# Layer 1's cross-attention: its first tiles placed away from the filler's memory, a norm in two halves, a third staging buffer, and a 2 MB load and two table loads moved

## The chip, the core and the metric

The kernel runs on one NeuronCore of a Trainium2 chip. The metric is device time in microseconds (us) of one execution: the median of three runs before the change is 2085.6 us (2083.99 to 2086.98). Five engines work side by side: TensorE (PE, with its weight loads shown as PEld), VectorE (DVE), ScalarE (ACT), GpSimd (POOL) and SyncE (SP), which here only issues DMAs. ACT and POOL issue DMAs too, each on its own queue (SPq, ACTq, POOLq in the profile).

## The reference

Four layers, each a cross-attention and a feed-forward network (FFN) with eight experts, on a residual `x` of 2 x 512 rows of 256, with a context of 2 x 1024 rows:

```python
x = x + L0_xattn(layernorm(x), ctx)
x = x + L0_ffn(layernorm(x))          # 8 experts, the best one per row, FFN 1024
x = x + L1_xattn(ctx, layernorm(x))   # 8 heads of 64
x = x + L1_ffn(layernorm(x))          # 8 experts of 512, and a shared one
x = x + L2_xattn(layernorm(x), ctx)
...
```

The change lies around layer 1's attention. Its reference, cut:

```python
def L1_xattn(x, latents, gamma_x, beta_x, gamma_l, beta_l, Wq, Wkv, Wo):
    xn = layer_norm(x, gamma_x, beta_x)          # the context
    ln = layer_norm(latents, gamma_l, beta_l)    # the residual, normalised a second time
    q = ln @ Wq
    k_x, v_x = split(xn @ Wkv)                   # 1024 rows of each batch
    k_l, v_l = split(ln @ Wkv)                   # 512 rows of each batch
    k = concat([rope_rotate(k_x), k_l])
    v = concat([v_x, v_l])
    return softmax(q * 64**-0.5 @ k.T) @ v @ Wo
```

So the keys and values of the context (`k_x`, `v_x`) depend on nothing but the inputs, and can be computed at any time before; the queries and 512 of each batch's keys and values need the residual that layer 0's FFN leaves.

## The kernel before

The residual `X` stays in SBUF as eight tiles of 128 rows (`[128, 8, 256]`, tiles 0 to 3 are batch 0). All matmuls are float32. Instructions are ordered by a scheduler that works on the program order and on dependencies; a call of `behind(x, y)` pins x behind y in an engine's stream. The scheduler also sees to the memory: a tile of a new pool that takes over the memory of an older tile waits for the older one's last use.

**Layer 0's FFN** (L1247 to L1301) routes the rows to experts. The function `moe` runs over pairs of slot tiles: indirect DMAs on POOL gather rows (`xs`, L648) and scatter results (`yd`, L660), PE computes `pa`, `pg`, `y`, and expert weights `w` arrive on SP's, ACT's and POOL's queues into the pool `L0g` (`ep`, four buffers).

**The filler.** Beside this FFN PE computes the keys and values of layer 1's context: `ahead1` makes, for each batch, 16 jobs (8 of keys, then 8 of values). A job is four matmuls of 128x512 from the transposed context `cT` and the weights `wkv` into a PSUM tile `pk` (L190 is the line of the helper `mm2`), a copy by ACT into a staging tile (`sk` for keys, L880; `sv` for values, L902; one tag with two buffers), and a 256 KB store that ACT issues into HBM (`kd`, `vd`). All 16 jobs of batch 0 run in `first_batch`, before the first pair; of batch 1, six run as `between` the pairs and ten behind the last pair (L1298).

**The end of the FFN.** Behind the ten jobs the results come back: four loads `yg` of 256 KB on SP (L831), eight additions into `X` on DVE (L868).

**Layer 1's attention** (L1302 to L1490) opens three pools, `L1c`, `L1k` and `L1t`, on the memory that the FFN's pools leave, the filler's `cT` and staging tiles among it. It normalises the eight tiles (`norm_of` twice: statistics on DVE L81, L82, square root on ACT L69, reciprocal on DVE L72; then `norm_to` L107 writes `xn`), transposes them on PE (16 transposes, L175, four to a PSUM tile) and scales them into `xT` on DVE or ACT (L182, L184). Then it runs over eight groups (batch, pair of heads). `fetch(n)` loads a group's keys `kT`, a copy with its halves exchanged (`turned`, four DMAs from `exchange`, L214) and values `v`; `prep(n)` is a generator that adds the residual's keys (`pk`), values (`pv`) and queries (`pq`, `qT`); `rotate` applies the rotary tables: DVE multiplies `turned` by the sine (L205), POOL multiplies `kT` by the cosine and adds (L206, L207). A stream of 6 steps a group follows: scores (`s`, L1367), maximum (`nm`, L1371), exp (`p`, L1374), transposes (L1388) and products (`o`, L1397). Small work is shared out between the steps as `pieces`.

**Later.** `cTr` is the transposed context that layer 2 reads, 2 MB; its load stands behind the definitions for later layers (L1898), and the scheduler issues it on SP behind `yg` and ahead of `fetch(0)`. In layer 1's FFN (L1894 to L1949) `sqrt_table()` is a small square root whose purpose is to have ACT's table of square roots loaded; it stands ahead of the keys and values for layer 2 (`keys16`, `values16`). ACT holds one table at a time: a change of function of another table shows as ACT_TABLE_LOAD.

## Time and profile before

| what | before |
|---|---|
| median of three runs | 2085.6 us |
| lowest and highest | 2083.99 and 2086.98 us |
| the profiled execution | 2082.45 us |
| its span, from first to last instruction | 2080.7 us |
| mean granted clock of TensorE | 0.978 |
| instructions | 29514 |
| HBM read and written | 232.70 and 24.82 MB |

The span is the profiled execution without the 1.75 us that lie around it. The page gives the busy time of each engine, then the span in 40 slices of 52 us; a digit is the busy share in tenths:

```profile
PE   7999999998998999999899899899999999999996
...
PEclk9999999999999999999999999899979999999998
DMA  4111111129884211100327241478300100289882
```

Counted from 0, slices 9 to 12 (468 to 676 us) hold the first filler batch, layer 0's FFN and the last ten jobs, slices 13 to 19 layer 1's attention. PEclk is the clock that TensorE was granted, in tenths. The places of the change, with their times in the trace:

| place | us |
|---|---|
| first batch of the filler, 16 jobs | up to 518 |
| last ten jobs of the filler | 647.5 to 669.2 |
| loads of yg issued | 651.04 to 653.9 |
| load of cTr issued | 654.09 |
| first load of kT issued | 669.29 |
| transposes of xn | 669.94 to 676.3 |
| first scores of attention 1 | 681.37 |
| layer 1's FFN, first expert load issued | 1015.48 |
| table load for the norm ahead of layer 2 | 1177.15 |

In lines of waits, "A <- B: t, n, l" says that the instruction group A stood idle for t us in n times, l the longest, until B ended.

### The profile page before, as it was taken

To read this page: it belongs to the slowest core of one execution; us is meant where nothing else is said; L and a number is where in the kernel's file an instruction comes from. 1 tells how busy PE (TensorE), PEld (TensorE's weight loads), DVE (VectorE), ACT (ScalarE), POOL (GpSimd) and SP (SyncE) were. 2 spreads that over 40 slices of the span, in tenths; PEclk is the share of its full clock that TensorE was granted. 3 is DMA by queue.
4 is the path that set the end of the run, shared out by engine and by line. 5 is a ranking of instruction groups with operands and counts; after the bars stand their busy time and mean duration, and the time that the engine had idled before them with its cause. 6 is when DMAs were issued, how large, how long until landed. Compare 5 with 4: busy or idle time off the path is not lost. (4 is left out here: it accounts for less than half of the span.)

```text
span 2080.7 us, 29514 instructions
## 1 busy us (share of the span) xinstructions
PE 1976.3 (95%) x11294; PEld 1147.5 (55%) x11294; DVE 1040.0 (50%) x2018; ACT 864.9 (42%) x1693; POOL 506.1 (24%) x500
## 2 busy tenths in 40 slices
PE   7999999998998999999899899899999999999996
PEld 3444444433666454555458644599833333488994
DVE  7666666782113566666531466410167767332223
ACT  4444444433112666656411344322225545624433
POOL 2132333310211212211213222453242311122220
PEclk9999999999999999999999999899979999999998
DMA  4111111129884211100327241478300100289882
GB/s 142 42 33 35 35 36 31 31 92 325 357 336 144 78 39 43 42 21 1 122 95 253 89 181 28 150 277 328 142 11 20 30 18 21 75 315 371 349 320 87
DMA packets 87911, 267.64 MB, mean 129 GB/s; under 512 B 23120, under 2 KB 55248, under 8 KB 79312
## 3 DMA queue, kind: packets, MB, share of 16 engines
q1 hardware_dynamic: 69040, 144.36, 20.9%
q0 software_dynamic: 10656, 106.57, 13.4%
q10 hardware_dynamic: 8064, 14.68, 1.9%
q8 instruction: 96, 1.57, 0.3%
q14 instruction: 55, 0.45, 0.1%
HBM read 232.70 MB, written 24.82 MB: 124 GB/s over the span
## 5 line engine op out<-in xcount | busy, mean ns | idle before, releaser
L1769 ACT ACTIVATE p<-s 128x512 f32<-128x512 f32 (+3 forms) x384 | 186.9, 545 | 154.5 <-PE s L1768 103.2
L1709 PE MATMUL s<-kT,qT 32*128 32x512 f32 (+3 forms) x768 | 201.8, 603 | 5.8 <-DVE mx L1718 1.9
L1768 PE MATMUL s<-qA,kT 32*128 32x512 f32 (+3 forms) x768 | 195.2, 593 | 0.5 <-DVE nm L1713 0.3
L1718 DVE TENSOR_REDUCE mx<-s 128x1 f32<-128x512 f32 x256 | 165.5, 694 | 53.3 <-PE s L1709 33.9
L190 PE MATMUL pa<-sT,w 128*128 128x128 f32 x1536 | 185.7, 275 | 0.8 <-issue 0.5
L190 PEld LDWEIGHTS pa<-sT,w 128*128 128x128 f32 x1536 | 181.6, 192 | 5.6 <-issue 2.8
L772 PE MATMUL y<-w,hT 128*128 128x256 f32 x768 | 175.9, 381 | 2.9 <-DVE hT L768 2.0
L1374 ACT ACTIVATE p<-s,nm 128x512 f32<-128x512 f32 x192 | 129.3, 686 | 80.9 <-DVE nm L1371 80.9
L1188 ACT ACTIVATE p<-s 128x1024 f32<-128x1024 f32 x128 | 124.1, 1021 | 89.8 <-PE s L1183 89.8
L207 POOL TENSOR_TENSOR kT<-kT,turned 128x512 f32<-128x512 f32 x62 | 100.9, 1634 | 226.2 <-DVE turned L205 198.4
L1189 DVE TENSOR_SCALAR p<-p 128x1024 f32<-128x1024 f32 x128 | 106.8, 842 | 96.2 <-ACT p L1188 96.2
L772 PEld LDWEIGHTS y<-w,hT 128*128 128x128 f32 x768 | 141.6, 190 | 22.2 <-DVE hT L768 3.2
L1371 DVE TENSOR_REDUCE nm<-s 128x2 f32<-128x1024 f32 x96 | 113.2, 1221 | 80.3 <-PE s L1367 80.3
L1194 DVE TENSOR_TENSOR acc<-acc,p 128x1024 f32<-128x1024 f32 x96 | 132.6, 1381 | 2.8
L768 DVE TENSOR_TENSOR hT<-act,pg 128x512 f32<-128x512 f32 x58 | 39.9, 687 | 177.5 <-PE pg L190 165.2
L1112 PE MATMUL o<-p,v 128*64 128x512 f32 x512 | 124.9, 606 | 2.6 <-DVE p L1189 2.6
L1183 PE MATMUL s<-qT,kT 64*128 64x512 f32 x512 | 127.2, 615 | 0.0
L660 POOL DMA_INDIRECT yd<-yo,slot_to x60 | 59.6, 993 | 264.8 <-ACT yo L819 124.1
L206 POOL TENSOR_TENSOR kT<-kT,cos 128x512 f32<-128x512 f32 x62 | 87.8, 1427 | 118.7 <-DMA turned<-kT 71.3
L1388 PEld LDWEIGHTS pt<-ident,p 128*128 128x128 f32 x768 | 84.1, 141 | 53.0 <-issue 20.0
L190 PE MATMUL pg<-sT,w 128*128 128x128 f32 x928 | 113.1, 275 | 0.0
L648 POOL DMA_INDIRECT xs<-xd,slot_of x60 | 57.8, 963 | 214.7 <-PE pt L654 124.5
(364 smaller groups left out, 3162.3 us busy)
## 6 DMA issues: line engine op xcount, KB each, us to landing
w<-in_L_experts_dram SPq DMA_DIRECT2D x8, 3200.0 KB
w<-in_L_experts_dram SPq DMA_DIRECT2D x6, 3072.0 KB
w<-in_L_experts_dram SPq DMA_DIRECT2D x8, 2048.0 KB
w<-in_L_experts_dram SPq DMA_DIRECT2D x8, 1536.0 KB
turned<-kT SPq DMA_DIRECT2D x60, 128.0 KB
kd<-sk ACTq DMA_DIRECT2D x28, 256.0 KB
yg<-yd SPq DMA_DIRECT2D x24, 256.0 KB
vd<-sv ACTq DMA_DIRECT2D x16, 256.0 KB
```

The lines of the kernel that those rows point to most:

```text
L190: nc.tensor.matmul(ps_ap, lhsT[:, dc, lcols], rhs[:, dc, rcols], start=(dc == 0), stop=(dc == 1))
L772: x = nc.tensor.matmul(y, hT[:, f, :], w2[:, f, :], start=(f == 0), stop=(f == FT - 1)).ins
L1112: nc.tensor.matmul(G[n]["o"][64 * j : 64 * j + 64, :], V[g, b][:, kt, pr * P + 64 * j : pr * P + 64 * j + 64], p[:, j, :], start=(kt == 0) ...
L1183: nc.tensor.matmul(s1[:, j, :], G[n]["kT"][r, kt * P : (kt + 1) * P], G[n]["qT"][r, :], start=True, stop=True)
L1188: last_exp[0] = nc.scalar.activation(p, s1, AF.Exp, scale=0.125).ins
L1194: nc.vector.tensor_add(G[n]["acc"], G[n]["acc"], p)
L1371: nc.vector.tensor_reduce(nm[:, qt, :, c], s1, AX.X, ALU.max, negate=True)
L1374: nc.scalar.activation(p[:, j, :], s1[:, j, :], AF.Exp, bias=nm[:, qt, j, c : c + 1], accum_out=l[:, qt, j, c : c + 1],)
L1709: nc.tensor.matmul(s1[:, :w], qT[r, qt * P : (qt + 1) * P], kT[r, c * 512 : c * 512 + w], start=True, stop=True)
L1718: G[n]["max"] = nc.vector.tensor_reduce(mx[:, qt, j, c : c + 1], s1, AX.X, ALU.max).ins
L1768: nc.tensor.matmul(s2[:, qs], kT[r, kt * P : (kt + 1) * P], qA[r, qs], start=True, stop=True)
L1769: G[n]["exp"] = nc.scalar.activation(p[:, j, qs], s2[:, qs], AF.Exp, scale=0.25).ins
```

## The change

- `ahead`/`ahead1`: the staging tag has three buffers for layer 1's keys and values (layer 2's keys keep two).
- Layer 0's FFN: the expert weights' pool is closed ahead of the pools around it. The attention's pools `L1c` and `L1k`, and a pool for `cTr`, are opened inside the FFN's scope on that memory (right side), while the filler's `cT` and staging tiles still live.
- The last ten jobs of the filler are split into nine and one. Between them, in program order, tiles 0 to 3 get their results, are normalised (`norm_of(X, 0, 4)`, `norm_to`) and transposed into `xT`; the last job is pinned behind these transposes on PE. Then tiles 4 to 7 get their results and their statistics.
- The other half's `norm_to` and transposes become `second_rows()`, three pieces in the attention's second step. The norm and the 16 transposes ahead of the attention are gone.
- `exp_table` loads ACT's table of exponentials behind the last square root of that norm. In layer 1's FFN `sqrt_table` stands behind `values16`, pinned behind the last copy of results.
- `cTr` is loaded behind the loads of `fetch(1)`, in the attention's first step.

```diff
@@ -62,11 +62,13 @@
             reason="order of the stream",
         )
 
+    scaled = [None]
+
     def recip_sqrt(src, n, scale, eps, after=None):
 
         r = small.tile([P, n], F32, tag=f"rsq{n}", name="rsq")
         nc.vector.tensor_scalar(r, src, scale, eps, ALU.mult, ALU.add)
-        x = nc.scalar.activation(r, r, AF.Sqrt).ins
+        x = scaled[0] = nc.scalar.activation(r, r, AF.Sqrt).ins
         if after is not None:
             behind(x, after)
         nc.vector.reciprocal(r, r)
@@ -157,6 +159,11 @@
             reason="order of the stream",
         )
 
+    def exp_table(after):
+
+        junk = small.tile([P, 1], F32, tag="junk", name="junk")
+        behind(nc.scalar.activation(junk, ones[:, 0:1], AF.Exp).ins, after)
+
     def layernorm(dst, src, n, twice=False):
         norm_to(dst, src, norm_of(src, 0, n, twice))
 
@@ -164,17 +171,17 @@
         for _ in turn_blocks(*args, **kw):
             pass
 
-    def turn_blocks(ps, dst, src, n, g=None, b=None, tag="mm", first=0):
+    def turn_blocks(ps, dst, src, n, g=None, b=None, tag="mm", first=0, **kw):
 
 
         for blk in range(first, n // 4):
             pair = ps.tile([P, 2, 512], F32, tag=tag, name="pt", bufs=2) if tag == "s" else None
             for dc in range(2):
-                pt = pair[:, dc, :] if tag == "s" else ps.tile([P, 512], F32, tag=tag, name="pt")
+                pt = pair[:, dc, :] if tag == "s" else ps.tile([P, 512], F32, tag=tag, name="pt", **kw)
                 for i in range(4):
-                    nc.tensor.transpose(
+                    x = nc.tensor.transpose(
                         pt[:, i * P : (i + 1) * P], src[:, blk * 4 + i, dc * P : (dc + 1) * P], ident
-                    )
+                    ).ins
                 to = dst[:, dc, blk * 512 : (blk + 1) * 512]
                 if g is None:
                     nc.scalar.copy(to, pt)
@@ -182,7 +189,7 @@
                     nc.vector.tensor_scalar(to, pt, g[:, dc : dc + 1], b[:, dc : dc + 1], ALU.mult, ALU.add)
                 else:
                     nc.scalar.activation(to, pt, AF.Identity, bias=b[:, dc : dc + 1], scale=g[:, dc : dc + 1])
-                yield
+                yield x
 
     def mm2(ps_ap, lhsT, lcols, rhs, rcols):
 
@@ -816,7 +823,7 @@
         return yd
 
     def plain(yo, y, *ws):
-        nc.scalar.copy(yo, y)
+        last_act[0] = nc.scalar.copy(yo, y).ins
 
     def results(pool, yd, t0, n, to=(None, None)):
 
@@ -875,7 +882,7 @@
             if job[0] == "k":
                 _, kd, j, col, cols, c0 = job
                 mm2(pk, w, cols, src, slice(c0, c0 + 512))
-                k = st.tile([P, 512], F32, tag="sk", name="sk", bufs=2)
+                k = st.tile([P, 512], F32, tag="sk", name="sk", bufs=2 if w.shape[2] == D else 3)
                 if bias is None:
                     nc.scalar.copy(k, pk)
                 else:
@@ -898,7 +905,7 @@
         def values(pv, kt):
             r = slice(b * S + kt * P, b * S + (kt + 1) * P)
             mm2(pv, cT, r, w, slice(512, 1024))
-            v = st.tile([P, 512], F32, tag="sk", name="sv", bufs=2)
+            v = st.tile([P, 512], F32, tag="sk", name="sv", bufs=3)
             nc.scalar.copy(v, pv)
             stored.append(nc.scalar.dma_start(vds["L1"][r, :], v).ins)
             stores.append(stored[-1])
@@ -944,7 +951,7 @@
         ahead(ps, None, None, None, [("v", n) for n in range(B * nkt // 2)], values)
         return copies
 
-    last_product = [None]
+    last_product, last_act = [None], [None]
 
     def value_tiles(pool, nkt):
 
@@ -1244,12 +1251,14 @@
     rw1 = load_rows(state, d["L1_ffn_router_wT"], "rw1")
     spread = load(pp, [P, P], d["c_spread"], "spread")
 
+    att = ExitStack()
     with (
         tc.tile_pool(name="L0f", bufs=1, reuse_waits="tile") as fp,
         tc.tile_pool(name="L0h", bufs=2, reuse_waits="tile") as hp,
-        tc.tile_pool(name="L0g", bufs=4, reuse_waits="tile") as ep,
         psum(2, "L0fps") as ps,
     ):
+        weights0 = ExitStack()
+        ep = weights0.enter_context(tc.tile_pool(name="L0g", bufs=4, reuse_waits="tile"))
         rb = load_bc(fp, d["L0_ffn_router_b"], "rb")
         xn = fp.tile([P, TT, D], F32, tag="xn", name="xn")
         mv = small.tile([P, TT, 2], F32, tag="mv8", name="mv")
@@ -1295,21 +1304,35 @@
                 ahead1(ps, hp, wkv, cT, 1, slice(2 * s - 2, 2 * s))
 
         yd = moe("L0", ps, hp, ep, xn, slots, 1024, AF.Silu, True, plain, first_batch, None, between)
-        ahead1(ps, hp, wkv, cT, 1, slice(6, None))
+        ahead1(ps, hp, wkv, cT, 1, slice(6, 15))
         yg = fp.tile([P, TT, D], F32, tag="xn", name="yg")
-        for t0 in (0, 4):
-            add_results(results(fp, yd, t0, 4, [yg[:, t0 : t0 + 4, :]]), [mp], X, range(4))
-
+        weights0.close()
+        ctxr = ExitStack()
+        crp = ctxr.enter_context(tc.tile_pool(name="ctxr", bufs=1, side="right", reuse_waits="tile"))
+        cTr = crp.tile([P, 2, B * S], F32, tag="cTr", name="cTr")
+        cp = att.enter_context(tc.tile_pool(name="L1c", bufs=1, side="right", reuse_waits="tile"))
+        kp = att.enter_context(tc.tile_pool(name="L1k", bufs=2, side="right", reuse_waits="tile"))
+        xT = cp.tile([P, 2, NT], F32, tag="xT", name="xT")
+        xn = cp.tile([P, TT, D], F32, tag="oT", name="xn")
+        got = [results(fp, yd, t0, 4, [yg[:, t0 : t0 + 4, :]]) for t0 in (0, 4)]
+        add_results(got[0], [mp], X, range(4))
+        norm = norm_of(X, 0, 4, True)
+        norm_to(xn, X, norm)
+        turned = list(turn_blocks(ps, xT, xn, 4, g_l, b_l))[-1]
+        start = len(nc.cur_bb.bb.instructions)
+        ahead1(ps, hp, wkv, cT, 1, slice(15, None))
+        for x in list(nc.cur_bb.bb.instructions)[start:]:
+            if x.engine == mybir.EngineType.PE:
+                behind(x, turned)
+        add_results(got[1], [mp], X, range(4))
+        norm = norm_of(X, 4, 4, True)
+        exp_table(scaled[0])
 
     with (
-        tc.tile_pool(name="L1c", bufs=1, reuse_waits="tile") as cp,
-        tc.tile_pool(name="L1k", bufs=2, reuse_waits="tile") as kp,
+        att,
         tc.tile_pool(name="L1t", bufs=2, reuse_waits="tile") as tmp,
         psum(1, "L1ps") as ps,
     ):
-        xT = cp.tile([P, 2, NT], F32, tag="xT", name="xT")
-        to_T(ps, xT, normed(cp, True, "oT"), TT, g_l, b_l, "s")
-
         wts = [cp.tile([P, 4, P], F32, tag=f"wt{i}", name=f"wt{i}") for i in range(2)]
         for w in wts:
             nc.gpsimd.memset(w, 0.0)
@@ -1351,9 +1374,15 @@
             kd = kds["L1"][n * P : (n + 1) * P, :]
             nc.sync.dma_start(kT[:, 0:S], kd)
             exchange(turned, kd, 32, 64)
-            nc.sync.dma_start(
+            return nc.sync.dma_start(
                 v[:, 0:8, :], vds["L1"][b * S : (b + 1) * S, pc].rearrange("(t p) f -> p t f", p=P)
-            )
+            ).ins
+
+        def second_rows():
+
+            norm_to(xn, X, norm)
+            yield
+            yield from turn_blocks(ps, xT, xn, TT, g_l, b_l, first=1, bufs=3)
 
         def scores(n, u):
             c, qt = u // 4, u % 4
@@ -1464,6 +1493,8 @@
 
 
             n, w = divmod(t, 6)
+            if t == 1:
+                pieces.add(second_rows(), 3)
             if n < len(groups):
                 for k in range(2):
                     scores(n, 2 * w + k)
@@ -1483,7 +1514,9 @@
                 if u == 5:
                     pieces.add(end(m), 2, True)
             if n + 1 < len(groups) and w == 0:
-                fetch(n + 1)
+                x = fetch(n + 1)
+                if n == 0:
+                    behind(nc.sync.dma_start(cTr, d["ctxT"].rearrange("(t p) f -> p t f", p=P)).ins, x)
             for k in range(4):
                 pieces.share(24 - 4 * w - k if n < len(groups) else 1)
                 if 0 < t <= 6 * len(groups):
@@ -1893,9 +1926,6 @@
 
     frp = ctx.enter_context(tc.tile_pool(name="front", bufs=1, reuse_waits="tile"))
     rw2 = load_rows(frp, d["L2_ffn_gate_wT"], "rw2")
-    ctxr = ExitStack()
-    crp = ctxr.enter_context(tc.tile_pool(name="ctxr", bufs=1, side="right", reuse_waits="tile"))
-    cTr = load_rows(crp, d["ctxT"], "cTr")
     pre, pp, loads, params = params16("L2", False, True)
     V = value_tiles(pp, 4)
 
@@ -1940,9 +1970,9 @@
         for t in range(TT):
             nc.vector.tensor_scalar(xn[:, t, :], xn[:, t, :], top[:, t : t + 1], None, ALU.mult)
         yd = moe("L1", ps, hp, ep, xn, slots, 512, AF.Silu, True, plain, shared)
-        sqrt_table()
         keys16(ps, fp, "L2", wk, bk, 4)
         copies = values16(ps, wv, 4, V)
+        sqrt_table(last_act[0])
         yg = fp.tile([P, TT, D], F32, tag="xT", name="yg")
         norm = landed(results(fp, yd, 0, 4, [yg[:, 0:4, :]]), None, copies[1])
         add_beside(results(fp, yd, 4, 4, [yg[:, 4:8, :]]), None)
```

## The prediction

> **What bounds the kernel now.** I read the page first: TensorE (PE) is busy for nearly the whole span, so only stretches in which it idles, or runs at half clock, can pay.
>
> ```profile
> PE 1976.3 (95%) x11294; PEld 1147.5 (55%) x11294; DVE 1040.0 (50%) x2018; ACT 864.9 (42%) x1693; POOL 506.1 (24%) x500
> ```
>
> Then the busy time by stretch (first figure: length; then each engine; last three: granted clock, DMA share, GB/s) around what the change touches: the last third of the first filler batch (485 to 520), the rest of layer 0's FFN (to 647), the seam into attention 1 (647 to 682), the attention.
>
> ```profile
> 485.00:500.00 15.00, 11.62 (x32) 4.61 (x31) 0.72 (x6) 2.34 (x4) 4.03 (x4) 1.00 0.90 309
> 500.00:520.00 20.00, 15.64 (x42) 5.29 (x42) 0.42 (x1) 6.22 (x10) 0.95 (x1) 1.00 0.92 310
> ...
> 545.00:647.00 102.00, 99.37 (x660) 76.27 (x656) 16.11 (x27) 15.24 (x29) 16.03 (x17) 1.00 0.71 291
> 647.00:660.00 13.00, 12.49 (x29) 5.62 (x30) 4.78 (x14) 4.21 (x6) 0.54 (x1) 1.00 0.72 245
> 660.00:671.00 11.00, 7.44 (x15) 2.73 (x13) 4.99 (x23) 3.25 (x7) 1.13 (x2) 0.84 0.58 207
> 671.00:682.00 11.00, 10.03 (x42) 5.88 (x44) 4.16 (x9) 4.03 (x6) 5.26 (x4) 0.84 1.05 303
> ...
> 700.00:1000.00 300.00, 299.25 (x1632) 156.67 (x1630) 193.01 (x262) 188.01 (x481) 51.55 (x39) 1.00 0.10 29
> ```
>
> The attention leaves 0.75 of 300 us idle: what starts it earlier ends it earlier, and what is put into it is paid in full. Two places have slack: the first batch (35 − 27.26 = 7.74 us idle) and the seam. The waits there (total us, times, longest), for the seam and then the batch:
>
> ```profile
> SPq L1352 <- PE pk L190: 14.6, 1, 14.6
> ```
>
> ```profile
> POOL wt L1315 <- PE pk L190: 21.7, 1, 21.7
> ...
> ACT sv L902 <- DMA vd<-sv: 6.1, 5, 2.7
> ...
> DVE xn L107 <- PE pk L190: 3.0, 1, 3.0
> ```
>
> ```profile
> ACT sk L880 <- DMA kd<-sk: 16.3, 6, 6.2
> ...
> ACT sv L902 <- DMA vd<-sv: 5.6, 3, 2.6
> ACT sv L902 <- DMA kd<-sk: 4.4, 2, 2.5
> ```
>
> In the seam three first users of attention 1's pools (the first key load, the memset, the normalised rows) wait for the filler's last matmul, whose memory they take over. In both places ACT's copy waits for a store that still holds one of two staging buffers. TensorE's own time line at the seam (start, us, ... [idle before]):
>
> ```profile
> 665.69 3.46 PE L190 MATMUL pk<-wkv,cT 128*128 128x512 f32 x4 [2.49 <-ACT sv L902]
> 669.94 0.33 PE L175 MATMUL pt<-ident,xn 128*128 128x128 f32 x1 [0.79 <-DVE xn L107]
> ...
> 674.11 1.73 PE L190 MATMUL pk<-xT,wkv 128*128 128x512 f32 x2
> ...
> 676.97 1.95 PE L190 MATMUL pv<-wkv,xT 128*128 128x128 f32 x16
> 678.76 1.88 PE L190 MATMUL pq<-xT,wq 128*128 128x512 f32 x4
> 681.37 1.99 PE L1367 MATMUL s<-kT,qT 64*128 64x512 f32 x8 [0.73 <-POOL kT L206]
> ```
>
> **The seam, part by part.** I follow it from the filler's start at 647.5 to the first scores, 681.37 before.
>
> Filler. A job is four 128x512 matmuls: eight of them took 3.7 us, so 1.84 a job; nine were over at 662.61 + 0.59 = 663.2 with PE hardly idle, and the third buffer leaves them there. The tenth waited 2.49 for ACT's copy, which waited for a store, and then ran at half clock (0.43 to 0.86 a matmul); its last pair ended at 669.15.
>
> First half's norm. The four loads of yg are issued at 651.0 to 653.9 and their eight additions ran from 654.47 to 659.0. Four tiles need two loads, four additions (0.42 each) and four statistics (0.40 + 0.17): about 657.6, then Sqrt at 657.9. DVE now runs the other half's additions and three of its statistics before it uses that Sqrt (4×0.42 + 3×0.57 = 3.4), and the second Sqrt follows at some 661.7. Four xn (0.40 each) take 662.8 to 664.2; they no longer wait for the filler. The eight transposes, one behind each xn, end at 664.6, an idle spell of about 0.5. The tenth job, pinned behind them, ends at 664.6 + 1.8 = 666.4.
>
> Eviction, the step I trust least. On DVE the half's xT eviction stands behind the other half's last norm steps, two products of turned with sin (0.69 each) and four xn (1.6): about 668.4 to 669.2. On ACT it stands behind the third Sqrt, the Exp table load (1.28) and two copies (0.59 each): 667.7 to 668.5. So PE idles from 666.4 to 669.2.
>
> First group. pk, pv and pq took 1.73, 1.95 and 1.88 with half a group's clock lost; together 5.6, then qT 0.60 and the gap of 0.73: first scores at 669.2 + 5.6 + 1.3 = 676.1, which is 5.3 earlier. kT's rotation was the last wait before the scores; its loads are now issued at 654.5 instead of 669.3, right behind yg, so POOL (two pairs of 1.43 and 1.63) ends near 670 and leaves that wait.
>
> Moved into the attention: eight transposes, two evictions, four xn. Eight transposes took 1.1 (669.94 to 673.2 with waits, 0.60 for a clean four): 1.2 us paid in full. DVE has a third of its time free there (193 of 300), so the rest is hidden; without that cover the four xn and one eviction would cost 1.6 + 0.8.
>
> Clock. Half clock held from 665.29 to 668.70 and 672.11 to 675.53. The new 2.8 us idle is longer than the 2.49 that came with the first spell, so I count one spell of 3.41, of which half, 1.7, is lost; 1.1 of it is already in the three rows taken. 0.6 more. Seam: 5.3 − 1.2 − 0.6 = **3.5**. Ends: with DVE's eviction in ACT's place and no half clock, 5.3 + 0.7 + 1.1 − 1.2 = 5.9; with two spells and 2 us later loads, −0.2.
>
> The Trainium skill (TensorE: Matmul & The Clock Gate, "What's actually happening") puts the drop to half clock behind one idle window of about 3.4 us. The trace shows the 3.41 us as the length of a slow spell, but a spell that began with 2.49 us of idle. By the page the 2.8 us would cost no clock and the seam would gain 5.2; by the row, 3.5. The row decides.
>
> **cTr's 2 MB load** was issued at 654.09 ahead of the first key loads, and goes behind the second group's. SP's queue behind it (kT, turned ×4, v) and the stores of the filler share its DMA time: the share was 1.05 at 671 to 682. It is used first at 1165.4, in a stretch with DMA share 0.10; the cover is 480 us, its price 0. What SP issues after it, group 2's loads, comes six steps later.
>
> **Third staging buffer in the first batch.** PE needs 1.84 us a job, but copies come every 2.6 (488.89, 492.10, ... 517.48). With stores deeper in flight the copies could follow PE: all 7.7 us back at most. But the DMA engines are at 0.90 and 0.92, loading 12 MB of expert weights between the stores, so only 0.10×15 + 0.08×20 = 3.1 us of their time is unused. Lower end 0: stores just wait longer. I take **3.0**, nearer the DMA's row. From 520 to 647 PE idles 0.91 + 2.63 us only, so what is won is carried to 647.5. Pair 1's weights landed near 527.5 for a start at 532.76; they hang on the same stores and come earlier with them, and the between jobs' waits could give 0 to 1.
>
> The Trainium skill (DMA: Bandwidth & Descriptors, "Issuing engines are not separate DMA queues") says that transfers of SP, ACT and GpSimd run on the same 16 engines and interleave. That speaks against the buffer: by it the gain ends at the 3.1 of unused share; by ACT's wait alone, 7.7.
>
> **Tables and order elsewhere, 0.** Exp: the load (1.28 at 681.29) lay under scores and maxima; exp came at 683.80 after DVE's maximum. Uncovered it costs 1.28, and in its new place it is already in ACT's chain above. Sqrt before layer 2: the load (1.28 at 1177.15) moves to where ACT idles 2.25, but norm_to also waited 0.66 for PE: 0 to 0.3 gained. Layer 1's FFN: before, two 1.5 MB expert loads stood first on SP, at 1015.48 (9.15 with a wait for POOL) ahead of the shared gate at 1024.73. Now gate, up and down go first, behind the weights' matmul at 1020.5, and down is rid of its wait for po (issued 1031.61). Three expert loads instead of two follow the xd stores at 1045 to 1047; 4.5 MB at the batch's 310 GB/s is 14.5 us, over by 1063, and the first routed tile comes near 1100 at DMA share 0.04. Uncovered: 5 us.
>
> Sum: 3.5 + 3.0 = 6.5. The profiled execution was 2082.45 (span 2080.7, 1.75 around it): 2075.95. It lies 3.15 below the median 2085.6, to which I apply the same difference: **2079.1**.
>
> **Rivals.** Differences under 0.2%, 4.2 us, are what this measurement can't tell from none.
> (a) Only one of the two gains comes: the batch is bound by DMA (gain 0 to 1), or the seam ends no sooner. For: DMA at 0.92; the eviction behind six other steps on DVE. Against: kT, xn and memset visibly wait only for memory. Gain 3.3, 2082.3; spread 2081.5 to 2085.
> (b) Both at their upper ends: 5.9 + 7.7 = 13.6 less 1 for PE's own limits: 2073. For: idle DMA time after 520 (share 0.34 in the last 5 us to 530) shows that weights could come later. Against: w2 and w3's blocks are issued between the stores.
> (c) Slower, one mechanism: SP's loads and ACT's stores share completion slots, so with 1.5 MB of group 0 loaded during the filler each store waits for a load and each load for a store; ACT's in-order queue then holds Sqrt and the copies, and PE stands. The waits of SP show the kind: SP's turned load waited 2.1 and its kT 2.0 for vd<-sv. Nine such alternations at 2 us are 18 us, against 6.5 + 4.2; it decides from about 11 us, that is six waits in series. Against: most of the slots' earlier transfers land by 663. Eight in series: 16 − 6.5 = 9.5 slower, 2095.
> (d) The change does nothing (scheduler's order undone): 2085.6. Against: PE's order does differ at the seam.
>
> **Chances.** Forecast 0.55 (2075 to 2081.4), (a) 0.20, (b) 0.06, (c) 0.14, (d) 0.05. Faster by over 0.2%: 0.55 + 0.06 + 0.02 of (a) = 0.63. Same: the rest of (a), (d) = 0.23. Slower: 0.14. Range 2073 to 2086.5: (c) and a rest lie outside. The likeliest case's own range is 2075 to 2081.4.
>
> **What would show it.** PE's idle time at 485 to 520 down from 7.7 to near 5 at DMA share about 1.0; first scores near 673 (3.0 + 5.3 before 681.37); kT's and xn's waits on pk gone; the xT eviction as last wait before pk; attention unchanged but for 1.2 us. Wrong if ACT's copies still come every 2.6 us, if ACT waits for turned or kT loads ahead of a store, or if expert loads are waited for near 1100.

## The result and the profile after

The kernel became slower: 2093.72 us (2088.39 to 2100.61, 18 runs) against 2084.68 us (2081.84 to 2089.37, 18 runs) for the kernel before on the same chip, a ratio of 1.0038 with a 95% interval of 1.0029 to 1.0048. The medians differ by 9.0 us and the ratio gives 8, where the prediction had 6.5 us less. The profiled execution took 2096.35 us (span 2094.6, mean granted clock 0.975; before 2080.7 and 0.978).

On the page, TensorE's instructions are the same in number and its busy time has grown by 3.5 us (1976.3 before), so most of the 14 us by which the two spans differ are idle time of TensorE:

```profile
PE 1979.8 (95%) x11294; PEld 1150.1 (55%) x11294; DVE 1048.6 (50%) x2026; ACT 864.9 (41%) x1696; POOL 506.7 (24%) x500
```

Busy time by stretch after, columns as before (stretch, length, PE, PEld, DVE, ACT, POOL, granted clock, DMA share, GB/s):

```profile
485.00:500.00 15.00, 12.58 (x30) 4.96 (x30) 0.72 (x6) 2.92 (x5) 4.03 (x4) 1.00 0.92 322
500.00:520.00 20.00, 14.75 (x46) 4.89 (x44) 0.42 (x1) 4.16 (x8) 0.95 (x1) 1.00 0.91 295
...
545.00:647.00 102.00, 99.81 (x664) 76.56 (x660) 16.09 (x27) 15.05 (x29) 15.61 (x16) 1.00 0.72 293
647.00:660.00 13.00, 11.56 (x27) 5.24 (x28) 2.93 (x10) 3.23 (x5) 1.95 (x3) 1.00 0.55 181
660.00:671.00 11.00, 8.11 (x22) 3.06 (x20) 9.04 (x38) 5.34 (x12) 2.40 (x2) 1.00 0.99 293
671.00:682.00 11.00, 5.74 (x19) 3.68 (x20) 5.21 (x5) 1.84 (x3) 4.26 (x4) 0.69 1.00 344
...
700.00:1000.00 300.00, 299.63 (x1628) 155.79 (x1626) 194.60 (x263) 188.55 (x483) 51.62 (x39) 1.00 0.10 29
```

The first batch (485 to 520) idles 7.67 us, as much as before (7.74). The seam (660 to 682) idles 8.15 us where it idled 4.53. The attention is as full as it was. Farther on, layer 1's FFN and the start of layer 2 show the other place, in the granted clock alone. Before, then after:

```profile
1018.00:1078.00 60.00, 51.02 (x190) 30.76 (x187) 25.23 (x84) 11.31 (x17) 16.85 (x23) 0.91 0.51 181
...
1163.00:1240.00 77.00, 70.58 (x434) 34.43 (x435) 45.37 (x171) 34.85 (x85) 20.46 (x38) 0.96 0.41 154
```

```profile
1018.00:1078.00 60.00, 51.38 (x182) 31.19 (x182) 24.43 (x82) 10.85 (x17) 17.10 (x23) 0.80 0.52 188
...
1163.00:1240.00 77.00, 69.72 (x391) 37.24 (x390) 38.77 (x142) 31.03 (x74) 16.97 (x30) 0.91 0.41 153
```

TensorE is busy nearly as long in both stretches, but gets fewer instructions done: it ran more of the time at half clock.

To place the time I use the lag: the start of a TensorE instruction after, less the start of the same instruction in the first profile of before, with the two traces' instructions paired in order (us of before along the top).

| | 465 | 545 | 640 | 740 | 1018 | 1078 | 1163 | 1240 | 2050 |
|---|---|---|---|---|---|---|---|---|---|
| after | −0.9 | 0.4 | 0.9 | 2.7 | 2.7 | 8.2 | 8.3 | 11.7 | 13.0 |

The seam itself, TensorE's time line after (start, us, count at the end, idle time ahead and its releaser in brackets):

```profile
665.84 1.73 PE L182 MATMUL pt<-ident,xn 128*128 128x128 f32 x8
...
668.47 1.98 PE L197 MATMUL pk<-wkv,cT 128*128 128x512 f32 x4 [0.89 <-ACT sv L909]
676.26 3.78 PE L197 MATMUL pk<-xT,wkv 128*128 128x512 f32 x4 [5.81 <-DVE xT L189]
...
684.76 1.99 PE L1396 MATMUL s<-kT,qT 64*128 64x512 f32 x8 [0.73 <-issue]
```

The order is the forecast one: eight transposes, the tenth job, then the first group behind the xT eviction. But the idle spell is 5.81 us, not 2.8. DVE's time line shows what the eviction stood behind:

```profile
665.38 1.38 DVE L109 TENSOR_SCALAR xn<-X,mv,rsq 128x256 f32<-128x256 f32 x4
...
668.55 0.18 DVE L74 RECIPROCAL rsq<-rsq 128x4 f32<-128x4 f32 x1 [1.52 <-ACT rsq L71]
...
669.04 1.29 DVE L212 TENSOR_TENSOR turned<-turned,sin 128x512 f32<-128x512 f32 x2
670.25 5.24 DVE L109 TENSOR_SCALAR xn<-X,mv,rsq 128x256 f32<-128x256 f32 x4
675.41 0.80 DVE L189 TENSOR_SCALAR xT<-pt,g_l,b_l 128x512 f32<-128x512 f32 x1
```

The first four xn take 1.38 us, the same four instructions on the other half's rows 5.24. POOL at that time:

```profile
669.86 1.59 POOL L214 TENSOR_TENSOR kT<-kT,turned 128x512 f32<-128x512 f32 x1 [6.20 <-DVE turned L212]
671.42 1.31 POOL L213 TENSOR_TENSOR kT<-kT,cos 128x512 f32<-128x512 f32 x1
672.81 1.26 POOL L214 TENSOR_TENSOR kT<-kT,turned 128x512 f32<-128x512 f32 x1
674.03 1.31 POOL L213 TENSOR_TENSOR kT<-kT,cos 128x512 f32<-128x512 f32 x1
```

Four instructions of POOL, back to back, from 669.86 to 675.34; four xn from 670.25 to 675.49, each as long as one of POOL's.

### The profile page after: what moved, and what is told of

It reads as the page before. It is cut to its first block, busy times and chain, and to the rows that moved or that the text cites. A ratio compares the mean times of both kernels' runs of the same rounds, so it can differ in the third digit from the quotient of the medians.

```text
span 2094.6 us, 29512 instructions
## 1 busy us (share of the span) xinstructions
PE 1979.8 (95%) x11294; PEld 1150.1 (55%) x11294; DVE 1048.6 (50%) x2026; ACT 864.9 (41%) x1696; POOL 506.7 (24%) x500
```

## The experiments

Three theories stood at the start: (1) the seam, DVE's xn held up by POOL's rotation ahead of the eviction (the port theory of the expectations); (2) the third staging buffer, which lets the first batch push something later; (3) something behind 1018, in layer 1's FFN. Each ratio is to the kernel before, timed on the same chip. A stage is the lag at its end less the lag at its start. The loss to the clock is the span times one less the mean granted clock, averaged over a kernel's timed runs: before 45.3 us (122 runs, standard error 0.3), after 49.9 (30 runs, 0.8), others with a standard error of 0.8 to 2.0. The mean spans of these runs of before and after differ by 6.9 us; 4.6 of them are this loss.

**Staging buffers: e1_two_buffers (after, with two) and e2_three_alone (before, with three).**

```diff
-                k = st.tile([P, 512], F32, tag="sk", name="sk", bufs=2 if w.shape[2] == D else 3)
+                k = st.tile([P, 512], F32, tag="sk", name="sk", bufs=2)
-            v = st.tile([P, 512], F32, tag="sk", name="sv", bufs=3)
+            v = st.tile([P, 512], F32, tag="sk", name="sv", bufs=2)
```

> The changed kernel with two staging buffers again, all else as changed. Buffer theory: the third buffer won 1.7 us up to 513 us (lag of TensorE against before from -0.76 to -2.42) and gave 2.9 back by 523 us, since ACT's Silu of the first pair then stood behind the last staged copy (519.93 against 517.48 before). With two buffers the lag at 541 us is -0.8 again, and the time falls by 1 to 2 us, to about 1.0033 of before. Rival (the forecast's own): the third buffer is worth up to 3 us, and without it the time rises by 2 to 3, to 1.005. Rival clock: what differs is only where half-clock spells fall; within 1 us of the changed kernel.

> The kernel before with the third staging buffer alone. Buffer theory: slower than before by 1 to 2 us (1.0005 to 1.001), PE idle at 485 to 520 still above 7 us, DMA share there about 0.91 as in both profiles. The forecast's own theory: faster by 2 to 3 us (0.9988).

e1: 2092.55 against 2086.57, 1.0026 (1.0010 to 1.0042). e2: 2083.91, 0.9998 (0.9983 to 1.0012). So in the times the buffer neither makes the loss nor pays. Where its 3.0 went is seen on ACT at the end of the first batch. Before:

```profile
518.45 1.28 ACT L704 ACT_TABLE_LOAD   x1 [0.39 <-ACT sv L902]
519.74 0.60 ACT L704 ACTIVATE act<-pa 128x512 f32<-128x512 f32 x1
...
521.66 0.59 ACT L902 COPY sv<-pk 128x512 f32<-128x512 f32 x1 [0.84 <-DMA vd<-sv]
```

After:

```profile
519.93 0.58 ACT L909 COPY sv<-pk 128x512 f32<-128x512 f32 x1 [2.82 <-DMA vd<-sv]
520.54 1.28 ACT L711 ACT_TABLE_LOAD   x1
521.83 1.08 ACT L711 ACTIVATE act<-pa 128x512 f32<-128x512 f32 x2
```

TensorE was 1.7 us earlier by 513 (lag −0.76 to −2.42). But ACT now takes the last copy ahead of Silu's table load and the first act; that copy waits 2.82 us for a store, and act comes 2.1 us later than before, so 2.9 us are given back by 531 (lag 0.4). Over 465 to 640, the ten profiles of kernels with three buffers stand at +2.8 in the mean, the nine with two at +0.9; e1's own missed its expectation, with a lag of 0.9 at 541, not −0.8. At the seam the third buffer paid, for which the forecast had counted nothing: the stage 640 to 740 is −3.8 in e2 where before has 0, −1.0 and 0.3, it is 3.1 in e1 where after has 0.3 in the mean, and −0.6 in e7, with two, where e6 has −4.3. These are one profile of each run; in the times none of it is clear of the uncertainty.

**The eviction's place: e3_evict_first and e8_rotation_held.** In e3 the second half's norm on DVE is put behind the first half's xT eviction:

```diff
+                    scaled_to[0] = nc.vector.tensor_scalar(to, pt, g[...], b[...], ALU.mult, ALU.add).ins
...
+            start, first = len(nc.cur_bb.bb.instructions), scaled_to[0]
             norm_to(xn, X, norm)
+            for x in list(nc.cur_bb.bb.instructions)[start:]:
+                if x.engine == mybir.EngineType.DVE:
+                    behind(x, first)
```

In e8 the xn stay ahead of the eviction, but POOL's rotation, all but its first instruction, waits for them:

```diff
+        norm_to(xn, X, norm)
+        normal = [x for x in nc.cur_bb.bb.instructions if x.engine == mybir.EngineType.DVE][-1]
+        start = len(nc.cur_bb.bb.instructions)
         rotate(*G[0]["kv"][:2], cos, sin)
+        held = [x for x in list(nc.cur_bb.bb.instructions)[start:] if x.engine == mybir.EngineType.Pool]
+        for x in held[1:]:
+            tc.add_manual_dep(x, normal.name, ...)
```

> The changed kernel with the second half's four xn pinned behind the first half's xT eviction on DVE. Port theory: the eviction, which started at 675.41 behind four xn that took 5.24 us beside POOL's rotation (1.31 each, as long as POOL's instructions, against 0.35 before), now starts at about 670.3; then ACT's eviction (ends 672.3) is last, the first scores come 4 us earlier (about 680.7) and the time falls by 3 to 5 us, to about 1.002 of before. Rival: ACT's chain and the late norm set the end anyway; the scores move by less than 1.5 us and the time stays at 1.0035 to 1.004. Rival clock: first scores earlier, but the time unchanged.

> The changed kernel with the second half's xn still ahead of the eviction, but POOL's rotation of kT (all but its first instruction) and the products with sin held until they are done. Port theory: the four xn take 1.4 to 1.6 us instead of 5.24, the eviction starts at about 671.7 instead of 675.41, first scores 3 to 4 us earlier than in the changed kernel. Rival (xn is slow for another reason, its memory or the operands): four xn still near 5 us with POOL idle, eviction not before 675.

e3: 2085.81, 1.0001 (0.9984 to 1.0017): the times show no loss any more. DVE and then TensorE in e3:

```profile
667.62 1.29 DVE L214 TENSOR_TENSOR turned<-turned,sin 128x512 f32<-128x512 f32 x2
668.83 0.80 DVE L189 TENSOR_SCALAR xT<-pt,g_l,b_l 128x512 f32<-128x512 f32 x1
669.56 4.54 DVE L109 TENSOR_SCALAR xn<-X,mv,rsq 128x256 f32<-128x256 f32 x4
```

```profile
669.69 1.13 PE L199 MATMUL pk<-xT,wkv 128*128 128x512 f32 x2 [0.65 <-DVE xT L189]
...
676.69 1.99 PE L1402 MATMUL s<-kT,qT 64*128 64x512 f32 x8 [0.73 <-issue]
```

The four xn are still slow, but nothing waits for them; the idle spell is 0.65 us and the first scores come at 676.69, against 676.1 in the forecast. That is 8 us ahead of after's first profile, twice what the expectation priced: the eviction came 6.6 us earlier, and the first group took 7.0 us in place of 8.5, since the 6.83 us of half clock from 674.09 didn't come. The stage 640 to 740 is −5.2. e8 (2088.21, 1.0013, 1.0001 to 1.0025) leaves the xn ahead of the eviction (only the products with sin now come behind them) and takes the neighbour away:

```profile
670.71 1.38 DVE L109 TENSOR_SCALAR xn<-X,mv,rsq 128x256 f32<-128x256 f32 x4
672.01 1.28 DVE L212 TENSOR_TENSOR turned<-turned,sin 128x512 f32<-128x512 f32 x2
673.21 0.80 DVE L189 TENSOR_SCALAR xT<-pt,g_l,b_l 128x512 f32<-128x512 f32 x1
```

The same four xn, the same data, 1.38 us: POOL alone had made them 5.24. The stage is −3.5. In time e8 lies below after, but the two intervals overlap, so this gain is likely and not shown.

**Layer 1's FFN: e4_ones_later.** There the shared expert's weights and the small tables are loaded first now (the table `one` is issued at 1027.45, before at 1033.56), and POOL's three products of kT with one no longer wait for a DMA, so they run beside the norm's eight xn. Before, then after:

```profile
1033.45 2.68 DVE L107 TENSOR_SCALAR xn<-X,mv,rsq 128x256 f32<-128x256 f32 x8
...
1038.18 4.65 POOL L1559 TENSOR_SCALAR kT<-kT,one 128x512 f32<-128x512 f32 x3 [5.05 <-DMA one<-in_c_one_dram]
```

```profile
1037.54 4.82 POOL L1592 TENSOR_SCALAR kT<-kT,one 128x512 f32<-128x512 f32 x3
...
1038.10 4.40 DVE L109 TENSOR_SCALAR xn<-X,mv,rsq 128x256 f32<-128x256 f32 x8
```

e4 holds POOL back until the last xn; e6_evict_ones has e3's and e4's edits, e7_evict_ones_two also two staging buffers.

```diff
-        keys = *standing16(pp, params[1], 4, 3, 0), maxima16(pp), 0
         xn = normed(fp, False)
+        normal = [x for x in nc.cur_bb.bb.instructions if x.engine == mybir.EngineType.DVE][-1]
+        start = len(nc.cur_bb.bb.instructions)
+        keys = *standing16(pp, params[1], 4, 3, 0), maxima16(pp), 0
+        for x in list(nc.cur_bb.bb.instructions)[start:]:
+            if x.engine == mybir.EngineType.Pool and "Memset" not in type(x).__name__:
+                tc.add_manual_dep(x, normal.name, ...)
```

> The changed kernel with POOL's three multiplications kT by one (4.82 us from 1037.54, beside the norm ahead of layer 1's FFN) held until that norm's last xn. Port theory: the eight xn take 2.7 us as before instead of 4.40, and the transposes behind them end about 1 us earlier; time lower by 0.5 to 1.5 us. Rival clock: the 5.6 us that were lost between 1025 and 1076 are half-clock spells (23.9 us of them against 10.2 before); xn shorter, time unchanged within 1 us.

> The two pins together: the second half's xn behind the first half's eviction, and POOL's kT by one behind the norm. Port theory: the gains add, first scores about 4.5 us earlier than before as with the first pin (676.7 there against 681.37), xn ahead of layer 1's FFN 2.7 us, 0.9985 of before (faster by 3 us). Rival: the 4 us won at the seam are lost to something else downstream that belongs to the change, and the time stays at 1.000.

> As the one before, with two staging buffers. Buffer theory: within 1.5 us of it, either way, since the DMA engines bound the first batch and the tenth job no longer waits at the seam. The forecast's theory: 2 to 3 us slower than with three.

e4: 2090.95, 1.0020 (1.0005 to 1.0034). The eight xn are back at 2.68 us and the stage 1018 to 1078 is +2.0 in place of +5.5, but the ratio's interval overlaps that of after, so a gain in time isn't shown. e6: 2085.82, 1.0000 (0.9986 to 1.0014), no better than e3 alone. e7: 2084.21, 0.9991 (0.9978 to 1.0005), the lowest ratio of all; that it beats the kernel before isn't shown either.

**Repeats: e5_after_again, e16_after_third, e17_after_fourth and, of before, e14_before_again, e15_before_third.**

> The changed kernel once more, for a second profile of it. What is of the kernel comes again: first scores 3 to 5 us later than before, four xn of 5.2 us at the seam, eight xn of about 4.4 ahead of layer 1's FFN. What is of the clock's phase does not: the 3.5 us lost near 1190 to 1205 and part of the 5.6 lost from 1025 to 1076 move or go. Rival (all is of the kernel): the same lags at the same places within 0.5 us.

> The kernel before once more, for its profile by stage. If the loss behind 1018 us is a matter of where the clock's windows fall in an execution, this kernel shows it too in some executions: 0 to 10 us later than the first profile behind 1018, by the position of its work in the window. If it belongs to the changed kernel, this one stays within 1.5 us.

> The changed kernel, a third profile. Windows theory: with its work at 0.79 to 0.98 of a window it loses less than 4 us behind 1018, elsewhere 5 to 10. Rival: 9 to 10 us whatever the position. In both the four xn at the seam take 5.2 to 5.5 us.

e5: 2091.03 against 2085.14, 1.0030 (1.0016 to 1.0044). One execution each: e14 2088.3, e15 2088.72, e16 2097.51, e17 2090.24 (the kernel before beside them 2082.6). The four xn at the seam took 5.2 to 5.3 us in all four profiles of after, and TensorE idled 4.8 to 5.8 us until the eviction behind them. The rest of e5's expectation missed: its first scores came at 681.65, 0.3 us later than before, and the losses of 5.4 us in 1018 to 1078 and 3.5 in 1163 to 1240 came again where they had been. e14 and e15 lost 6.5 and 4.4 us behind 1018, so such a loss is not the changed kernel's alone. e16 and e17 fell at places of the window for which 5 to 10 us were expected and lost 9.0 and 6.2; neither fell at 0.79 to 0.98, so the other half of that expectation stayed untried. By stage:

| stage | after | mean | before | mean |
|---|---|---|---|---|
| 465 to 640 | 1.8, 1.6, 4.3, 1.7 | 2.4 | 0, 1.1, −0.7 | 0.1 |
| 640 to 740, the seam | 1.8, −1.2, 0.8, −0.2 | 0.3 | 0, −1.0, 0.3 | −0.2 |
| 740 to 1018 | 0, 0, −0.1, −0.1 | 0 | 0, 0, 0.1 | 0 |
| 1018 to 2050 | 10.3, 9.3, 9.0, 6.2 | 8.7 | 0, 6.5, 4.4 | 3.6 |

The differences, 2.3 + 0.5 + 5.1 = 7.9, come near the 8 us of the times, from few profiles that spread by 4 to 6.5 us in the last stage. The first profile of before was a lucky one behind 1018, so the 13.0 of lag in the first pair of profiles overstates the loss.

**Delay or alignment: e9_work_1_7, e10_work_3_4, e12_after_2_6, e13_before_0_9.** Behind 1018 TensorE's instructions are the same. If only their position against the clock's windows counts, some added work ahead of them should change the loss to the clock by more, or less, than the work. e9 and e10 compute the second group's pq two and three times over in the kernel before; e12 and e13 add three single matmuls to after and one to before.

```diff
+            for _ in range(2 if n == 1 else 1):
                 mm2(pq, wq, pc, xT, ...)
```

```diff
+            for _ in range(3 if n == 1 else 0):
+                nc.tensor.matmul(pq, wq[:, 0, pc], xT[:, 0, ...], start=True, stop=True)
```

> The kernel before, with the matmuls of one group's queries (pq of the second group, 1.7 us) done twice, so that everything behind 690 us comes half a window of 3.41 us later. Alignment theory (what the granted clock takes later depends on where the work falls in windows of 3.41 us): lag 1.7 at 740 us and another figure at the end, off by more than 1 us from 1.7; mean loss to the clock (span times one minus the granted clock) other than before's 45 us by 3 or more. Rival (the later loss of the changed kernel has its own cause, and a delay is only a delay): lag and time 1.7 higher, loss to the clock as before's within 1.5.

> The same with these matmuls three times: 3.4 us, one whole window. Alignment theory: loss to the clock as before's, the time 3.4 us higher. Rival: the same here; the two runs together tell them apart. A third possibility, any delay costs more than itself: time higher by 5 us or more in both.

> The changed kernel with three extra matmuls (2.6 us, three quarters of a window of 3.41) ahead of the second group's queries, overwritten by these. Alignment theory: the work behind the attention then falls in the windows as it does in the kernel before (in the profiles so far the later loss was 0 to 4 us where the work stood at 0.79 to 0.98 of a window and 6 to 10 where it stood at 0.63 to 0.72); the loss to the clock falls from 50 to about 46 us, and the time rises by less than 1 us over the changed kernel's 2092.8 in spite of 2.6 us more work. Rival (the loss belongs to the changed kernel's own work): loss stays at 50, time 2095.4.

> The kernel before with one such extra matmul (0.86 us, a quarter of a window). Alignment theory: its work then falls at about 0.66 of a window, where the changed kernel's did; loss to the clock from 45 to about 49, time about 4 to 5 us higher for 0.86 us of work. Rival: loss as before's within 1.5, time 0.9 higher.

| kernel | ratio | loss to the clock |
|---|---|---|
| e9, before + 1.7 us | 1.0010 (0.9996 to 1.0023) | 48.0 |
| e10, before + 3.4 us | 1.0013 (0.9999 to 1.0027) | 44.2 |
| e12, after + 2.6 us | 1.0037 (1.0022 to 1.0051) | 47.8 |
| e13, before + 0.9 us | 0.9999 (0.9982 to 1.0015) | 45.0 |

The standard error of a loss is 0.8 to 1.4 here, and the intervals of the ratios are some 3 us wide to each side. e9 and e10 go the way that alignment has it: with half a window of added work the loss is 2.7 ± 1.4 us above before's, with a whole one 1.1 ± 1.1 below (3.41 us is the length of a window); their times fit the rival as well. e12's loss fell by half of what was expected (47.8, not 46), and 2.6 us more or less are not resolved between its ratio and after's. e13 speaks against: no loss was added. One thing more speaks against: the place of the windows differs from execution to execution, so a fixed delay can move a mean only if these places cluster. In the 19 profiles they do (none lies between 0.38 and 0.56), and no run shows why. Alignment stays a possibility, not a finding.

**e11_tail_third**: e3's edit, the third buffer in the last ten jobs only, and Exp's table load behind ACT's own xT eviction.

```diff
-                k = st.tile([P, 512], F32, tag="sk", name="sk", bufs=2 if w.shape[2] == D else 3)
+                k = staged("sk")
...
-        exp_table(scaled[0])
+        exp_table(scaled_on[0])
```

> The changed kernel with the second half's xn behind the eviction, the third staging buffer only for the last ten jobs, and the table of exponentials loaded behind ACT's xT eviction. By the profiles so far: no loss at 515 to 545 (lag -0.9 at 640, as with two buffers), first scores 1.3 us earlier than the first pin alone gave against its own start, so about 5 us earlier than before; lag at 740 about -5 to -6; time 2080 to 2082, 0.998 of before. Rival: 0.9995 to 1.000, the clock gives it back.

2088.36, 1.0000 (0.9988 to 1.0013). The stage 640 to 740 was the best of all, −5.3, and in the same profile 9.6 us were lost behind 1018, so there the rival held. Over its timed runs the loss to the clock is 46.2 ± 1.4, near before's 45.3, so the clock explains that one profile and not why the times show no gain.

## Why the prediction was wrong

By stage the forecast was off in three places: up to 640 it had 3.0 us won and the profiles 2.3 lost, at the seam 3.5 won and 0.5 lost, behind 1018 nothing and 5.1 lost.

**The step whose failure the experiments show is the eviction**, the one called least trusted: "on DVE the half's xT eviction stands behind ... four xn (1.6): about 668.4 to 669.2". The order was right. The price of the xn, 0.40 each, came from a row of before in which POOL ran nothing but a memset of 1.13 us. Beside POOL's rotation they took 5.24 instead of 1.6, 3.6 us more. The rest of the delay: the filler's lag of 0.9 at 640, and 2.5 us in the norm (its first Sqrt at 661.31 instead of 657.9, since one pair of yg's loads landed 1.6 us late and the other half's additions and statistics came ahead; its last Sqrt at 668.31, behind a copy of ACT that waited 2.21 for vd<-sv). The eviction ended at 676.21, which is 669.2 + 0.9 + 2.5 + 3.6. The first group then took 8.5 instead of 6.9 us, at clock 0.69. So the first scores came at 684.76, not 676.1; in stages, +0.5 instead of −3.5 us. Two readings were off without weight: pk's 1.73 is the row of two of its four matmuls, and POOL's instructions took 1.26 to 1.59, not 1.43 and 1.63.

The trace of before had a sign of it in the very row that was priced. Its first two xn, beside POOL's memset, took 0.69 us each, the other six 0.40 (duration ns: least, median, most; then POOL's time line):

```profile
L107 DVE TENSOR_SCALAR xn<-X,mv,rsq x8: 395/407/694, 669.2 to 672.0; 128x256 f32<-128x256 f32 x8
```

```profile
669.22 1.13 POOL L1315 MEMSET wt<- 128x512 f32 x2 [21.68 <-PE pk L190]
```

A larger price stood in a row far from the seam, attention 0's product on DVE:

```profile
L1189 DVE TENSOR_SCALAR p<-p x128: 662/689/1761, 36.1 to 455.4; 128x1024 f32<-128x1024 f32 x128
```

One form, one size, 0.66 to 1.76 us: all 23 that took over 0.8 us ran beside POOL's instructions. The forecast itself moved POOL's rotation from behind 673 to before 670, that is onto the xn, and didn't ask what DVE does beside it.

The Trainium skill (SBUF — State Buffer, "Who interferes with whom") says that VectorE's tensor_scalar and copy can use a second pair of ports that belongs to GpSimd too, that whoever issues first holds it for its whole instruction while the other stands still, and that a tensor_reduce never contends. At the seam the traces agree: each xn ended 0.15 us behind one of POOL's instructions and took as long (1.31 us). For the tensor_reduce no run here is a test: only 5 of attention 1's 96 ran beside POOL, and they read PSUM. That rule spoke against the change, and the prediction didn't weigh it.

**The third buffer** was sized at 3.0 us up to 640. There the profiles of after lost 2.3. At the seam the pairs above suggest a gain of some 3 us by the buffer that the forecast hadn't counted, and the times show neither. The bound from DMA was right in kind: the share stayed at 0.91 to 0.92, and TensorE's idle time at 7.67 us. The step that failed is "what is won is carried to 647.5": ACT's Silu stood behind a copy that waited for a store.

**Layer 1's FFN and the tables, costed at 0**, were the third miss: the loads' new order frees POOL's products to run beside the xn, 4.40 us in place of 2.68. With POOL held back (e4) the stage 1018 to 1078 lost 2.0 us, in after's four profiles 2.9 to 5.6.

**Right:** the waits of the key load and of xn on the filler's last matmul are gone; the order on TensorE; the attention, full with 299.63 of 300 us; the 2 MB load at 0; the Sqrt ahead of layer 2 (the lag is 8.2 to 8.3 from 1078 to 1182, past its norm); no wait for expert loads near 1100. Of the rivals, the slower one had 2095, near the measured time by luck. It named SP's and ACT's waits for each other: ACT's copies at 519.93 and 667.83 did wait 2.8 and 2.2 us for stores, but that didn't decide it: e3 has no loss left in the times and keeps waits of 1.65 and 1.43 us in both places.

**Open:** 5.1 of the 7.9 us arise behind 1018, and 4.1 of these in 1018 to 1078 (4.9 in the mean of after, 0.8 of before), where the change moved the loads and POOL's products. The lost time there is half clock: in after's first profile the stage lost 5.9 us more to it than in before's and idled 0.5 us less. At like places of the clock's windows (0.57 to 0.76, last section) five profiles with the xn beside POOL lost 2.9 to 5.6 us in this stage, three with the xn free (e4, e9, e14) 2.0 to 2.2; at other places the xn beside POOL cost 0.1 to 0.3 (e3, e8), 1.0 (e12) and 3.6 (e1). So the two together are the likely cause, and no times show it: e4's interval overlaps after's, and e6 is no better than e3. e3 and e8, which touch the seam alone, lost only 3.7 and 0.2 us behind 1018 in one profile each, and their mean loss to the clock, 45.0 and 46.4 (± 1.8 and 2.0), lies below after's 49.9. Whether the mended seam does that, and why after stood at a bad place in all four profiles, stays open.

## What to carry to other kernels

Before an instruction of DVE is moved or its neighbour on POOL starts earlier, look at the least and the longest duration of its form in the trace: a wide spread says that its price depends on what runs beside it, and the sum needs the price beside the new neighbour. Where the first user of a result and work of no hurry share an in-order engine, order the first user ahead by hand; here that one dependency was worth 0.3 to 0.4% of the time (after 1.0038 and 1.0030, with it 1.0001). And where TensorE waits in many short spells, executions of one kernel differed by up to 6.5 us over the same work (3.4 of it half clock), so a gain of that size has to be shown in times, not in one profile.

## What the runs showed of the hardware

Price of DVE beside POOL: a 128x256 fp32 tensor_scalar 0.35 us alone, 1.31 beside back-to-back 128x512 tensor_tensor of POOL; 128x1024 0.69 and about 1.75. POOL's own took 1.26 to 1.31 beside these xn, as alone, but up to 2.12 beside the 128x1024.

The half clock: in all 19 profiles I cut the span into windows of 3.413 us, on the grid on which all half-clock spells of a profile begin. From 465 to 2050 us, a full-clock window with TensorE busy for less than 0.40 of it was followed by half clock in 61 of 61 cases; 0.40 to 0.45, 31 of 37; 0.45 to 0.75, 105 of 421; 0.75 and more, 30 of 7859. So some 2 us of idle inside one window cost half of the next, and the same 2 us across two windows mostly cost nothing. The grid's place differs from execution to execution. For each profile I take the place of the grid, less the lag of the work at 1018, as a share of a window (the expectations call it the place of the work). At 0.57 to 0.76 (8 profiles, after's four included), 6.2 to 10.3 us were lost from 1018 to 2050; at 0.79 to 0.98 (7), −0.1 to 3.7; at 0.12 to 0.37 (4), 1.5 to 7.9. This order was found in the same profiles that it sorts, and the kernels sort them nearly as well: before and its variants −0.1 to 6.5, after and its variants with the seam as it was 5.0 to 10.3. The Trainium skill (TensorE: Matmul & The Clock Gate, "What's actually happening") gives one idle window of about 3.4 us as the cause of the drop and has the window run free of the kernel; the second agrees with the moving grid, and for the first the runs show a little over half a window as enough.
